# A three-layer edge-convolution kernel: two of the lone group's products between its first nodes, PSUM pools laid in another order, two of the last pairs in plain float32, and a second queue for the last stores

## The chip, the cores and the metric

The kernel runs on one core of one Trainium2 chip. The metric is the device time of one execution in microseconds (us); lower is better. A core has five engines with their own instruction queues: PE (TensorE, matrix products), DVE (VectorE), ACT (ScalarE), POOL (GpSimd) and SP (SyncE, which issues transfers here). They run side by side and wait for each other by semaphores. "PEld" in a profile is PE's load of the stationary operand.

## The reference, cut to what matters

There are 2500 nodes with 256 features and 80000 edges, sorted by their target. A layer is an edge convolution with a mean over a node's incoming edges:

```python
h = jnp.maximum(_layernorm(x), 0.0)
xs = [h]
for W, b in ((W0, b0), (W1, b1), (W2, b2)):
    xi, xj = h[dst], h[src]
    m = jnp.concatenate([xi, xj - xi], axis=-1) @ W + b          # 80000 x 256
    s = segment_sum(m, dst, 2500); cnt = segment_sum(1, dst, 2500)
    h = relu(s / maximum(cnt, 1)[:, None])
    xs.append(h)
return x + jnp.concatenate(xs, axis=-1) @ Wf + bf
```

With A[source, target] the number of edges between two nodes, and W split into an upper half Wa and a lower half Wb, a node's sum is its column of A times (h Wb + b), plus cnt times its own h (Wa - Wb). So nothing has to be done per edge once A is there.

## The kernel before

All of it is in `by_windows` (a general routine, `general`, stands behind a flag that is read at the very end and isn't entered for these inputs). Nodes lie in 20 tiles of 128, taken as Q = 10 pairs. Instructions on the engines stand in the order in which the code issues them (the wrappers `PEo`, `DVEo`, `ACTo`, `SPo` of class `InOrder`, line 282, which is why nearly every line of the profile is L282; the tile names tell the groups apart).

**Start and layer 0 (0 to 206 us).** A list of two-letter acts, `order` (line 893), is run by `perform`: loads, layer norm of node pairs (`st`, `rs`, `sq`, `sc`, `N`: statistics, variance, root, scales, normalization), transposition to feature-major `hT` (`T`, `R`), the search for the edges' blocks (`first`, `next`, `pick`, `pk`, `sg`, `se`, `ge`) and the first products. In `order`, `sc0` is `scales(0)` on DVE and `pick` is `find_rows`, three DVE instructions whose result PE multiplies in `pk`; `warm12` puts twelve idle products on PE ahead of the first `pk`. Then A is built from one-hot products, in five groups of target columns, four of 504 and one of 486 (group 4, the "lone" group), and stored to DRAM as bf16 (`a_dram`), while PE multiplies the previous group.

**Layers 1 and 2.** `hT` holds features times the node's edge count, and `share` is one over the count. Each layer has two stages.

The *node stage* is a loop over i in 0..Q+1 (line 1298). For pair i, `Nodes.multiply` makes 12 products of 128x512 in float32r: per tile, h times [Wb | the layer's part of Wf], where each operand is split in three float32r parts by `Split` (ACT makes the high part, DVE the low one and then the third, "across") and by `Forms` for the weights, and a product is high x high + low x ... + across x ... (`times`). `Nodes.parts` scales the Wb half into `zh` and `zl` (high and low part of z), and `add_to_acc` adds the Wf half to the output sum `acc`. `combine` and `sums` make four combinations of a pair's z. `split(order[i + 2])` makes the split of the next pair but one. Between the pairs, two pairs behind (LAG = 2), `lone.multiply` adds eight products of 128x486 of z with the lone group's counts to two PSUM banks from the pool `ps_two`. `lone.end` closes them with the group's own term: four plain float32 products of `wt` (Wa - Wb) with `hT`, and a ReLU each. The nodes' banks come from the pool `ps_six` (six banks).

The *stream* (70 steps) multiplies z with the four other groups, as two pairs of groups by seven products in place of eight, with banks from both pools in turn. In its last steps (`tick`) the next stage's `Forms` and its first splits are made: for layer 2 those of the first three pairs in the order, for the final stage those of the first four.

**The final stage (457 to 476 us)** is a loop over the pairs in the order 8, 9, 0, 1, 2, 3, 7, 6, 5, 4: 12 products of 128x256 by `times` into the two halves of one bank, two `add_to_acc` on DVE, two stores of 128 rows from SP, and the `split` of a pair some places on. After it, each engine loads the flag `missing` (L1372), branches (L1373) past `general`, and meets the others at closing barriers (L1397).

```python
for i, q in enumerate(order):
    po, sp = bank(), splits.pop(q)
    for k in range(2):
        times(po[:, k * D:(k + 1) * D], sp, k, coming[0])
    for k in range(2):
        t = 2 * q + k
        add_to_acc(t, po[:, k * D:(k + 1) * D])
        n = P if t < NT - 1 else LAST
        SPo.dma_start(out[t * P:t * P + n, :], acc[:n, t, :])
    for k in order[i + 1:i + 4]:
        if k not in splits:
            split(k)
```

Of the kernel before, what the change touches and what calls it, by code (L numbers as in the profile page):

```python
# [12 lines left out]
PSUM = bass.MemoryType.PSUM  # L13
# [300 lines left out]
def by_windows(ctx: ExitStack, tc: tile.TileContext, x, src, dst, Ws, bs, Wf, bf, out, missing):  # L314
    nc = tc.nc
    PE, DVE, ACT, POOL, SP = nc.tensor, nc.vector, nc.scalar, nc.gpsimd, nc.sync
    PEo, DVEo, POOLo, ACTo, SPo = (InOrder(tc, e) for e in (PE, DVE, POOL, ACT, SP))
    P = 128
    N, D = x.shape
# [4 lines left out]
    L = len(Ws)  # L324
    DC = D // P
# [22 lines left out]
    Q = NT // 2  # L348
# [23 lines left out]
    def bank():  # L372
        return ps[-1].tile([P, 512], F32, name="bank")


    acc = const.tile([P, NT, D], F32, name="acc")
    hT = const.tile([P, DC, NP], F32, name="hT")

    zh = const.tile([P, 2, Q * D + 32], F32R, name="zh")
# [17 lines left out]
    lim = const.tile([P, WG], F32, name="lim")  # L397
# [16 lines left out]
    def tile_of(z, t):  # L414
        return z[:, t % 2, t // 2 * D:(t // 2 + 1) * D]
# [20 lines left out]
    ws = [None] * L  # L436
    wfs = [None] * (L + 1)
    raws = [None] * (L + 1)

    def load_wb(l, queue=SP):  # L440
        raws[l] = wpool.tile([P, DC, 2, D], F32, name="wbf", bufs=1)
        ws[l] = wpool.tile([P, DC, D], F32, name="wt"), raws[l][:, :, 0, :]
        queue.dma_start(ws[l][1], Ws[l][D:2 * D, :].rearrange("(c p) d -> p c d", p=P))

    def load_wt(l, queue=SP):
        queue.dma_start(ws[l][0], Ws[l][0:D, :].rearrange("(c p) d -> p c d", p=P))

    def load_wf(l, queue=SP):
        if l == L:
            raws[l] = wpool.tile([P, DC, 2, D], F32, name="wbf", bufs=1)  # L450
        wfs[l] = raws[l][:, :, 1, :]
        queue.dma_start(wfs[l], Wf[l * D:(l + 1) * D, :].rearrange("(c p) d -> p c d", p=P))
# [22 lines left out]
    def load_b(l, queue=SP):  # L475
        queue.dma_start(brow[PAD:PAD + 1, l % 2, :], bs[l].rearrange("(o d) -> o d", o=1))
# [28 lines left out]
    first = pp.tile([P, 1], F32, name="first")  # L505
    after = pp.tile([P, 1], F32, name="after")
    behind = pp.tile([P, WG * P], F32, name="behind")
    pick = pp.tile([P, WG * P], F32R, name="pick")
# [334 lines left out]
    def layer(l, g, a, own, PE=PE, ACT=ACT):  # L843
# [47 lines left out]
        "warm": keep_warm,  # L891
    }
    order = """
        long warm8 lim io first next dstr st0 rs0 sq0 sc0 warm12 N0 pick pk00 sg00 pk01 sg01 st1 T0 pk11 R0 st4 rs1 sq1 pk30 se0
        sg11 sc1 Z0 pk20 N1 st5 sg30 ge0 T1 st6 R1 rs3 F0 sg20 pk21 sq3 st7 pk10 H0 F1 rs4 st3 sq4 sc4 G0 st9
        sc3 L0 sg21 N6 pk31 ka0 kb0 Z1 N5 st8 N7 G1 T6 rs5 sg10 sg31 km0 T5 se1 kt0 R6 H1 st2 F6 sq5 sc5 k10 k20
        rs2 Z6 ge1 L1 T7 B0 R5 R7 Z5 B1 C0 B2 ka1 G6 H6 N9 H5 C1 T9 F7 E0 ge2 kb1 R9 sq2 km1 E1 kt1 C2 B3 k21 Z9
# [39 lines left out]
    splits, coming = {}, []  # L937
# [4 lines left out]
    def flat(l):  # L942
        return raws[l].rearrange("p c t d -> p c (t d)") if l < L else wfs[l]
# [57 lines left out]
    for g in range(NG):  # L1001
        at = {}
        own = LATE
        if g + 1 < NG:
# [5 lines left out]
            if g:  # L1010
                own = [u + 1 - i for i, u in enumerate(sorted(at)[1:5])]
# [20 lines left out]
    first_layer.close()  # L1032

    banks_of.close()
    ps_two = ctx.enter_context(tc.tile_pool(name="ps_two", bufs=2, space=PSUM))
    ps_six = ctx.enter_context(tc.tile_pool(name="ps_six", bufs=6, space=PSUM))
    turn_of = [0]

    def bank():
# [22 lines left out]
    def combine(to, x):  # L1062
        DVEo.tensor_sub(to[:, M3:S5 + 1, :], x[:, 1::2, :], x[:, 0:2, :])
        DVEo.tensor_sub(to[:, S2, :], to[:, M3, :], x[:, 3, :])
        DVEo.tensor_add(to[:, M4, :], to[:, S2, :], x[:, 2, :])
# [4 lines left out]
    def times(to, split, i, forms):  # L1070
        for c in range(DC):
            for k in range(3):
                PEo.matmul(to, split.parts[k][:, c, i * P:(i + 1) * P], forms.parts[k][:, c, :],
                           start=(c == 0 and k == 0), stop=(c == DC - 1 and k == 2))

    def add_to_acc(t, po):
        DVEo.scalar_tensor_tensor(acc[:, t, :], po, share[:, t:t + 1], acc[:, t, :], op0=OP.mult, op1=OP.add)

    class Nodes:
# [4 lines left out]
        def multiply(self, split, forms):  # L1084
            self.banks = [bank(), bank()]
            for i in range(2):
                times(self.banks[i], split, i, forms)
# [117 lines left out]
    class Alone:  # L1205
# [12 lines left out]
        def multiply(self, p):  # L1218
            block = self.blocks.pop(p)
            for i in range(2):  # L1220
                t = 2 * self.order[p] + i
                for o in range(DC):
                    for z in (zh, zl):
                        unit[0] = PEo.matmul(self.to[o], tile_of(z, t)[:, o * P:(o + 1) * P], block[:, i, :self.n],
                                             start=(p == 0 and i == 0 and z is zh), stop=False)

        def end(self):
            for o in range(DC):
                for c in range(DC):
                    PEo.matmul(self.to[o], ws[self.l][0][:, c, o * P:(o + 1) * P],  # L1230
                               hT[:, c, self.c0:self.c0 + self.n], start=False, stop=(c == DC - 1))
            for o in range(DC):
                ACTo.activation(hT[:, o, self.c0:self.c0 + self.n], self.to[o], AF.Relu)

# [2 lines left out]
    def load_alone(k, order):  # L1237
        c = order[2 * k] // 2
        st = stage.tile([P, 8 * GS], BF16, name="staged").rearrange("p (t n) -> p t n", n=GS)[:, :4, :]
        SPo.dma_start(st, a_dram[alone][:, 4 * c:4 * c + 4, :])  # L1240
        loaded[k] = st
# [39 lines left out]
                tick(n)  # L1281

    AHEAD_H = 2
    LAG = 2
    orders = [None, list(range(Q)), [8, 9, 0, 1, 2, 3, 7, 6, 5, 4], [8, 9, 0, 1, 2, 3, 7, 6, 5, 4]]
    def split(q):
        tile_ = stage.tile([P, 4 * GS], F32R, name="staged")
        Split(q, [tile_[:, k * 2 * D:(k + 1) * 2 * D] for k in range(3)])

    for l in range(1, L):  # L1290
        order = orders[l]
        lone = Alone(l, order)
        if l == 1:
            load_alone(0, order)
            split(order[2])
        pending = []
        stream = Stream(l)
        for i in range(Q + LAG):
            if 0 < i <= Q:
                lone.make(i - 1)  # L1300
            if i < Q:
                q = order[i]
                n = Nodes(l, q)
                n.multiply(splits.pop(q), coming[0])
                if i + AHEAD_H < Q and i % 2 == 1:
                    load_alone((i + 1) // 2, order)
                n.parts()
                n.combine()
                if i + AHEAD_H < Q and order[i + AHEAD_H] not in splits:
                    split(order[i + AHEAD_H])  # L1310
                pending.append(n)
            if i and pending:
                pending.pop(0).sums()
            if i >= LAG:
                lone.multiply(i - LAG)
            if i == Q - 1:
                load_alone(Q // 2 - 1, order)
                stream.load(3)
        stream.make(2)
        lone.end()  # L1320
        turn_of[0] = 0
        if l + 1 < L:
            load_b(l + 1, SPo)
            load_wb(l + 1, SPo)
            load_wt(l + 1, SPo)
        load_wf(l + 1, SPo)
        after = orders[l + 1]

        def tick(n):
            if n == 3:  # L1330
                combine(wsum, ws[l][0].rearrange("p c (o n) -> p (c o) n", o=2))
            if n == 40 and l + 1 < L:
                DVEo.tensor_sub(ws[l + 1][0], ws[l + 1][0], ws[l + 1][1])
            if n in (49, 56):
                split(after[(n - 49) // 7])
            if n == 63 and l + 1 < L:
                load_alone(0, after)
            if n in ((65,) if l + 1 < L else (63, 65)):
                split(after[2 + (65 - n) // 2])
            if n == 64:  # L1340
                raw = flat(l + 1)
                coming[:] = [Forms(raw, [raw[:, c, :] for c in range(DC)])]
                coming[0].high()
                coming[0].low()
            if n == 66:
                coming[0].across()
            if n == 67:
                coming[0].last()

        stream.run(tick)  # L1350

    order = orders[L]
    for i, q in enumerate(order):
        po, sp = bank(), splits.pop(q)
        for k in range(2):
            times(po[:, k * D:(k + 1) * D], sp, k, coming[0])
        for k in range(2):
            t = 2 * q + k
            add_to_acc(t, po[:, k * D:(k + 1) * D])
            n = P if t < NT - 1 else LAST  # L1360
            SPo.dma_start(out[t * P:t * P + n, :], acc[:n, t, :])
        for k in order[i + 1:i + 4]:
            if k not in splits:
                split(k)


# [36 lines left out]
```

## Time and profile before

| | |
|---|---|
| Median of 3 runs (lowest, highest) | 483.75 us (483.29, 484.77) |
| Profiled execution: its own time | 483.3 us |
| Its span | 481.5 us |
| Around the span | 1.8 us |
| PE, DVE, ACT, POOL busy | 469.0, 387.5, 303.5, 43.2 us |
| Start and layer 0 | 0 to 206 us |
| Layer 1: node stage, stream | 206 to 249, 249 to 332 us |
| Layer 2: node stage, stream | 332 to 376, 376 to 457 us |
| Final stage, and end of the program | 457 to 476, 476 to 481.5 us |

How to read it: a busy time is the part of the span in which an engine had an instruction under way; matrix products are pipelined, so a row of products that start every 0.23 us may each be shown as 0.39 us long. In lists in order of time, a row has its start, its length, engine, line, operation, the tiles written and read, their shapes and a count; "[0.33 <-DVE staged]" says that the engine was idle for 0.33 us before it and that a DVE instruction on the tile `staged` ended the wait. A "q" behind an engine is its instruction queue: issues of transfers, branches and semaphore waits. The tile `staged` is also what the splits of the later pairs are written to, `block` holds the `Forms` and the counts as float32r, `wbf` the weights Wb and the part of Wf, `pz` the first layer's plain products.

### The profile page before, as it was taken

Reading aid. Unit: us, or ns where it says so; the run is one execution under the profiler, and the core shown is the slowest. Engines: PE = TensorE matmul, PEld = TensorE weight load, DVE = VectorE, ACT = ScalarE, POOL = GpSimd, SP = SyncE. Lnnn points to the kernel's source line nnn. Section 1 sums busy time; section 2 is a strip of 40 time slices with the busy share of each in tenths; the row PEclk is TensorE's granted clock in tenths of the full one; section 3 lists DMA queues with packets and bytes.
Section 4 is the critical chain, followed back from the end, with each engine's and each line's share of the span. In section 5 each row is a group of like instructions: output and inputs, shape, how many; then the busy total and the mean of one; then the engine's idle time right before and its main releaser. Section 6 shows DMA issues by size and latency. Waiting matters only on the chain.

```text
span 481.5 us, 7530 instructions
## 1 busy us (share of the span) xinstructions
PE 469.0 (97%) x2736; PEld 367.8 (76%) x2736; DVE 387.5 (80%) x840; ACT 303.5 (63%) x530; POOL 43.2 (9%) x66
## 2 busy tenths in 40 slices
PE   8999999999999999999999999999999999999993
PEld 4888888677777778777887867877788787688693
DVE  8999988998889884559986838876999586669885
ACT  5676677564644336077868857766877796588340
POOL 3683016100101001000000000000000000000000
PEclk9999999999999999999999999999999999999998
DMA  9310088990641906522186552011124754220033
GB/s 285 111 52 1 2 166 164 197 197 2 128 89 26 189 3 136 100 76 80 43 292 246 174 172 85 3 43 38 49 52 160 283 179 166 86 87 0 2 105 115
DMA packets 21848, 52.76 MB, mean 110 GB/s; under 512 B 1977, under 2 KB 12170, under 8 KB 21770
## 3 DMA queue, kind: packets, MB, share of 16 engines
q1 hardware_dynamic: 15018, 34.57, 21.6%
q0 software_dynamic: 5856, 16.51, 18.0%
q10 hardware_dynamic: 928, 1.11, 0.8%
q8 instruction: 23, 0.38, 0.3%
q14 instruction: 23, 0.19, 0.1%
HBM read 36.72 MB, written 16.10 MB: 110 GB/s over the span
## 4 chain that ended last, share of the span: by engine, by line
PE 88%; DVE 6%; POOL 3%; ACT 1%; issue 1%; DVEq 0%; ACTq 0%; POOLq 0%
PE bank L282 84%; PE pz L282 4%; DVE staged L282 2%; DVE acc L282 2%; POOL acc L282 2%; POOL ed L282 1%; DVE zl L282 1%; POOL es L282 1%; DVE tmp L282 0%; DVE st L282 0%; PE turned L282 0%; ACT zh L282 0%; ACT hT L282 0%; ACT junk L282 0%; DVE mv L282 0%
## 5 line engine op out<-in xcount | busy, mean ns | idle before, releaser
L282 ACT CAST block<-staged 128x1008 fp32r<-128x1008 bf16 x120 | 117.9, 1031 | 16.7 <-DVE staged L282 6.3
L282 ACT CAST a<-bank 128x480 fp32r<-128x480 f32 (+1 forms) x105 | 52.9, 565 | 59.6 <-PE bank L282 59.6
L282 PE MATMUL bank<-a,zh 128*128 128x504 f32 (+1 forms) x200 | 84.3, 421 | 0.0
L282 DVE TENSOR_TENSOR one_m<-iota_m,key_m 128x1024 bf16<-128x1024 bf16 (+1 forms) x105 | 71.8, 684 | 14.2 <-PE bank L282 14.1
L282 PE MATMUL bank<-block,zh 128*128 128x504 f32 (+1 forms) x200 | 82.9, 415 | 0.0
L282 PE MATMUL bank<-a,zl 128*128 128x504 f32 (+1 forms) x200 | 77.8, 389 | 0.0
L282 PE MATMUL bank<-block,zl 128*128 128x504 f32 (+1 forms) x200 | 77.3, 386 | 0.0
L282 PE MATMUL bank<-block,staged 128*128 128x512 f32 (+1 forms) x336 | 69.8, 358 | 1.9 <-DVE staged L282 1.9
L282 PE MATMUL bank<-block,sh 128*128 128x504 f32 x160 | 69.0, 431 | 0.0
L282 DVE TENSOR_TENSOR one_n<-iota_n,key_n 128x480 bf16<-128x480 bf16 (+1 forms) x210 | 66.7, 357 | 0.0
L282 PEld LDWEIGHTS bank<-block,staged 128*128 128x128 f32 x336 | 55.4, 188 | 13.4 <-DVE staged L282 3.9
L282 PE MATMUL bank<-block,sl 128*128 128x504 f32 x160 | 62.6, 391 | 0.0
L282 DVE TENSOR_TENSOR block<-staged 128x1008 fp32r<-128x1008 bf16 x40 | 46.9, 1204 | 5.3 <-PE bank L282 3.9
L282 PEld LDWEIGHTS <-one_m 128*128 128x128 bf16 x834 | 39.1, 98 | 10.0 <-issue 3.2
L282 PEld LDWEIGHTS bank<-a,zh 128*128 128x128 f32 x200 | 37.8, 189 | 10.7 <-issue 2.6
L282 PEld LDWEIGHTS bank<-block,zh 128*128 128x128 f32 x200 | 37.6, 188 | 10.4 <-issue 2.5
L282 PEld LDWEIGHTS bank<-block,zl 128*128 128x128 f32 x200 | 37.6, 188 | 10.3 <-issue 3.2
L282 PE MATMUL bank<-one_n,one_m 128*128 128x120 bf16 x834 | 44.2, 208 | 0.4 <-DVE one_n L282 0.4
L282 PEld LDWEIGHTS bank<-a,zl 128*128 128x128 f32 x200 | 37.7, 189 | 9.0 <-issue 2.6
L282 DVE TENSOR_TENSOR staged<-staged 128x1008 bf16<-128x1008 bf16 x40 | 27.1, 678 | 20.8 <-ACT block L282 20.4
L282 PE MATMUL pz<-wbf,hT 128*128 128x256 f32 x160 | 38.4, 385 | 0.1
L282 PEld LDWEIGHTS bank<-block,sh 128*128 128x128 f32 x160 | 30.1, 188 | 10.4 <-issue 3.5
(152 smaller groups left out, 593.2 us busy)
## 6 DMA issues: line engine op xcount, KB each, us to landing
staged<-a_dram SPq DMA_DIRECT2D x52, 504.0 KB, 4.1
a_dram<-a POOLq DMA_DIRECT2D x20, 630.0 KB, 9.3
out_dram<-acc SPq DMA_DIRECT2D x19, 128.0 KB, 2.0
acc<-in_x_dram POOLq DMA_DIRECT2D x3, 640.0 KB, 11.8
wbf<-in_L_gnn_Wf_dram SPq DMA_DIRECT2D x4, 256.0 KB, 7.3
acc<-in_x_dram SPq DMA_DIRECT2D x1, 896.0 KB, 9.5
acc<-in_x_dram ACTq DMA_DIRECT2D x1, 768.0 KB, 7.1
wbf<-in_L_gnn_W_dram SPq DMA_DIRECT2D x3, 256.0 KB
```

Of the source, the lines that this page charges most:

```text
L282: return self.tc.keep_in_program_order(call(*args, **kwargs))
```

## The change

- In `order`, `pick` moves from behind `sc0` to ahead of it.
- `ps_six` is opened before `ps_two`, so the nodes' banks are the first six and the lone group's the last two.
- Of the lone group's four own products, the two with the first half of the features move from `lone.end` into the node stage: `lone.own(0, 0)` behind the products of the second pair, `lone.own(1, 0)` behind those of the third. They now open the accumulation.
- In the final stage, pairs 2 and 7 (`PLAIN`) are multiplied in plain float32: four products per pair of `hT` with the unsplit `wfs[L]`, and no split is made for them. Because `wfs[L]` has to stay whole, the last `Forms` keeps its rest in the unused half of the weight tile.
- The last pair's two halves get a bank each.
- The second store of each of the last two pairs is issued by ACT, not SP.

```diff
--- before.py
+++ after.py
@@ -891,7 +891,7 @@
         "warm": keep_warm,
     }
     order = """
-        long warm8 lim io first next dstr st0 rs0 sq0 sc0 warm12 N0 pick pk00 sg00 pk01 sg01 st1 T0 pk11 R0 st4 rs1 sq1 pk30 se0
+        long warm8 lim io first next dstr st0 rs0 sq0 pick sc0 warm12 N0 pk00 sg00 pk01 sg01 st1 T0 pk11 R0 st4 rs1 sq1 pk30 se0
         sg11 sc1 Z0 pk20 N1 st5 sg30 ge0 T1 st6 R1 rs3 F0 sg20 pk21 sq3 st7 pk10 H0 F1 rs4 st3 sq4 sc4 G0 st9
         sc3 L0 sg21 N6 pk31 ka0 kb0 Z1 N5 st8 N7 G1 T6 rs5 sg10 sg31 km0 T5 se1 kt0 R6 H1 st2 F6 sq5 sc5 k10 k20
         rs2 Z6 ge1 L1 T7 B0 R5 R7 Z5 B1 C0 B2 ka1 G6 H6 N9 H5 C1 T9 F7 E0 ge2 kb1 R9 sq2 km1 E1 kt1 C2 B3 k21 Z9
@@ -1032,8 +1032,8 @@
     first_layer.close()
 
     banks_of.close()
+    ps_six = ctx.enter_context(tc.tile_pool(name="ps_six", bufs=6, space=PSUM))
     ps_two = ctx.enter_context(tc.tile_pool(name="ps_two", bufs=2, space=PSUM))
-    ps_six = ctx.enter_context(tc.tile_pool(name="ps_six", bufs=6, space=PSUM))
     turn_of = [0]
 
     def bank():
@@ -1222,13 +1222,15 @@
                 for o in range(DC):
                     for z in (zh, zl):
                         unit[0] = PEo.matmul(self.to[o], tile_of(z, t)[:, o * P:(o + 1) * P], block[:, i, :self.n],
-                                             start=(p == 0 and i == 0 and z is zh), stop=False)
+                                             start=False, stop=False)
+
+        def own(self, o, c):
+            PEo.matmul(self.to[o], ws[self.l][0][:, c, o * P:(o + 1) * P],
+                       hT[:, c, self.c0:self.c0 + self.n], start=(c == 0), stop=(c == DC - 1))
 
         def end(self):
             for o in range(DC):
-                for c in range(DC):
-                    PEo.matmul(self.to[o], ws[self.l][0][:, c, o * P:(o + 1) * P],
-                               hT[:, c, self.c0:self.c0 + self.n], start=False, stop=(c == DC - 1))
+                self.own(o, 1)
             for o in range(DC):
                 ACTo.activation(hT[:, o, self.c0:self.c0 + self.n], self.to[o], AF.Relu)
 
@@ -1281,6 +1283,7 @@
                 tick(n)
 
     AHEAD_H = 2
+    PLAIN = (2, 7)
     LAG = 2
     orders = [None, list(range(Q)), [8, 9, 0, 1, 2, 3, 7, 6, 5, 4], [8, 9, 0, 1, 2, 3, 7, 6, 5, 4]]
     def split(q):
@@ -1311,6 +1314,8 @@
                 pending.append(n)
             if i and pending:
                 pending.pop(0).sums()
+            if 0 < i <= DC:
+                lone.own(i - 1, 0)
             if i >= LAG:
                 lone.multiply(i - LAG)
             if i == Q - 1:
@@ -1339,7 +1344,7 @@
                 split(after[2 + (65 - n) // 2])
             if n == 64:
                 raw = flat(l + 1)
-                coming[:] = [Forms(raw, [raw[:, c, :] for c in range(DC)])]
+                coming[:] = [Forms(raw, [raw[:, c, :] if l + 1 < L else raws[L][:, c, 0, :] for c in range(DC)])]
                 coming[0].high()
                 coming[0].low()
             if n == 66:
@@ -1351,16 +1356,22 @@
 
     order = orders[L]
     for i, q in enumerate(order):
-        po, sp = bank(), splits.pop(q)
+        po = bank()
+        po = [po[:, :D], bank()[:, :D] if i == Q - 1 else po[:, D:]]
         for k in range(2):
-            times(po[:, k * D:(k + 1) * D], sp, k, coming[0])
+            if q in PLAIN:
+                for c in range(DC):
+                    PEo.matmul(po[k], hT[:, c, (2 * q + k) * P:(2 * q + k + 1) * P], wfs[L][:, c, :],
+                               start=(c == 0), stop=(c == DC - 1))
+            else:
+                times(po[k], splits[q], k, coming[0])
         for k in range(2):
             t = 2 * q + k
-            add_to_acc(t, po[:, k * D:(k + 1) * D])
+            add_to_acc(t, po[k])
             n = P if t < NT - 1 else LAST
-            SPo.dma_start(out[t * P:t * P + n, :], acc[:n, t, :])
+            (ACTo if i >= Q - 2 and k else SPo).dma_start(out[t * P:t * P + n, :], acc[:n, t, :])
         for k in order[i + 1:i + 4]:
-            if k not in splits:
+            if k not in splits and k not in PLAIN:
                 split(k)
```

## The prediction

> **What bounds the kernel now.** I read the page's busy rows and chain first, then busy time by stage, then the instructions in order of time in the stages that the change touches.
>
> ```profile
> PE 469.0 (97%) x2736; PEld 367.8 (76%) x2736; DVE 387.5 (80%) x840; ACT 303.5 (63%) x530; POOL 43.2 (9%) x66
> PE 88%; DVE 6%; POOL 3%; ACT 1%; issue 1%; DVEq 0%; ACTq 0%; POOLq 0%
> ```
>
> PE is busy 97% and makes 88% of the chain that ended last. A gain must take work from PE, fill one of its holes, or shorten a stretch that PE doesn't own. Busy time by stage (length; then PE, PEld, DVE, ACT, POOL) finds the holes:
>
> ```profile
> 332.00:376.00 44.00, 43.44 (x189) 35.21 (x189) 37.42 (x83) 33.72 (x57) 0.00 (x0) 1.00 0.34 105
> 376.00:457.00 81.00, 81.00 (x326) 60.67 (x325) 59.14 (x82) 58.11 (x68) 0.00 (x0) 1.00 0.31 107
> 457.00:476.00 19.00, 16.27 (x123) 15.03 (x121) 17.04 (x34) 5.66 (x8) 0.00 (x0) 1.00 0.35 115
> 476.00:482.00 6.00, 0.00 (x0) 0.00 (x0) 0.00 (x0) 0.00 (x0) 0.00 (x0) 0.66 0.23 76
> ```
>
> The streams are solid. Layer 2's node stage lacks 0.6, the final stage 2.7, and the last 6 us hold no computing. The node stage's hole, in order of time:
>
> ```profile
> 341.51 0.69 DVE L282 TENSOR_TENSOR staged<-hT,staged 128x512 fp32r<-128x512 f32 x1
> 341.54 0.39 PE L282 MATMUL bank<-block,staged 128*128 128x512 f32 x1
> ...
> 342.23 0.69 DVE L282 SCALAR_TENSOR_TENSOR staged<-staged 128x512 fp32r<-128x512 f32 x1
> ...
> 342.25 0.49 PE L282 MATMUL bank<-block,staged 128*128 128x512 f32 x1 [0.33 <-DVE staged L282]
> ...
> 342.98 0.73 PE L282 MATMUL bank<-block,staged 128*128 128x512 f32 x2 [0.23 <-DVE staged L282]
> ```
>
> The fourth pair's `Split` is late: DVE makes its second and third part as PE asks for them. Starts lie 0.71 and 0.73 apart where 0.23 is the pace: 0.97 lost. The final stage on DVE:
>
> ```profile
> 466.11 0.69 DVE L282 SCALAR_TENSOR_TENSOR staged<-staged 128x512 fp32r<-128x512 f32 x1
> 466.72 0.87 DVE L282 SCALAR_TENSOR_TENSOR acc<-bank,share,acc 128x256 f32<-128x256 f32 x2
> 467.51 0.68 DVE L282 TENSOR_TENSOR staged<-hT,staged 128x512 fp32r<-128x512 f32 x1
> 468.22 0.69 DVE L282 SCALAR_TENSOR_TENSOR staged<-staged 128x512 fp32r<-128x512 f32 x1
> 468.83 0.87 DVE L282 SCALAR_TENSOR_TENSOR acc<-bank,share,acc 128x256 f32<-128x256 f32 x2
> ```
>
> DVE never idles here: a pair costs 2.11 (466.72 to 468.83), 0.78 for two adds and 1.33 for one split, while PE's 12 products take 1.42 (pairs' adds began at 458.96 and 460.38). PE's weight loads wait 0.54 a pair. DVE bounds this stage. Then the end:
>
> ```profile
> L282 SPq DMA_DIRECT2D out_dram<-acc x6: 332/392/1697, 473.6 to 477.3; - x6
> L1373 SPq EVENT_SEMAPHORE  x8: 17/17/17, 478.3 to 479.2; - x8
> L1373 ACTq COMPARE_BRANCH  x1: 50/50/50, 466.9 to 466.9; - x1
> L1373 ACTq EVENT_SEMAPHORE  x1: 17/17/17, 469.6 to 469.6; - x1
> L1397 SPq DRAIN  x3: 7/7/131, 480.4 to 480.9; - x3
> ```
>
> The six last stores queue on SP; one issue took 1.70, so the last went out at 477.3, though DVE's last add began at 475.1 (call it R). SP's wait for landings ends at 479.2, it reaches the closing barrier at 480.4 to 480.6, and the span ends at 481.5, R+6.4. ACT had left long before.
>
> **What the Trainium skill says.** "FP8 and Floating Point Precision", TensorE Precision Notes: true float32 takes four passes. The trace agrees: the chain has the eight 128x256 records of a float32 `product` in 1.73, 0.43 per product, against 0.117 for a float32r one, 3.7 times. "DMA: Bandwidth & Descriptors", Issuing engines are not separate DMA queues: a second issuing engine only saves the sequencer's time to initiate, usually small. Here that time is 0.3 to 0.4, once 1.70. "Runtime: NRT & Kernel Launch", Instruction fetch mechanics: a taken branch out of the loaded window waits for a DMA fetch. The trace agrees: ACT's branch takes 0.05 but its next instruction comes 2.7 later; DVE's comes 3.1 later, and PE's branch alone takes 4.0. "PSUM — Partial Sum Buffer", PSUM bank collisions: two engines must not touch one bank at once; accordingly a pair's two adds follow all twelve products here.
>
> **The change, part by part.**
>
> *Lone group's own products.* In each of two layers, two of four float32 products move from `end` to behind the second and third pair of nodes. Each is two records 0.41 apart, 0.81 (eight in 202.11 to 205.5). PE's total stays. In layer 2 they put 1.63 ahead of the fourth pair, which then starts at 341.54+1.63 = 343.17; its parts are ready at 342.25 and 342.98. The split's inputs come from pair 1, whose products precede the moved ones, so DVE isn't later. The hole closes: **-1.0**. Behind the products on PE stand pair 3 and the lone group's products; their readers on DVE and ACT are 0.8 to 1.6 later once, and catch up because a node costs PE 12x0.234+8x0.22 = 4.57 and DVE some 4.4. What the products read (`wt`, lone columns of `hT`) was finished before the stage. In layer 1 no such hole shows: 0, since the two nodes given before are taken from `end`. Range -1.1 to -0.7 if a later split is late instead.
>
> *PSUM banks.* The first pair now lands in a bank that layer 0's last group held. PE waits for that group's last ReLU at 206.20 already (0.67), and the built program's semaphore wait is the same; the other banks were emptied before. 0, from -0.1 to +0.2.
>
> *Start.* `find_rows` (0.15+0.49+0.75, some 1.2 in all) goes ahead of `scales` on DVE. `pick` is ready at 7.4 instead of 7.9, but PE's warm-up products hold it to 8.4: nothing gained. `normalize` of pair 0 on ACT moves from 6.60 to about 7.8 and ends at 8.9, just when PE wants it (8.90) and ACT wants `count_half` (8.95). 0, from -0.1 to +0.2.
>
> *Two plain pairs.* Pairs 2 and 7, fifth and seventh in the order, lose their splits (2x1.33 on DVE, 2x0.63 on ACT) and cost PE 1.73 instead of 1.42. Follow it in the old clock: the fourth pair ends on PE at 460.34+2x1.42 = 463.18, the fifth (plain) at 464.91. DVE, done before that with the split of pair 3, runs from 464.95 without a hole: three times (two adds 0.78, one split 1.33) is 6.33, then six adds 0.39 apart; the last starts at 464.95+6.33+1.95 = 473.23 against 475.08. PE finishes pairs at 466.3, 468.1, 469.5 and 470.9, each before DVE wants it; the last waits about 0.3 for its split. **-1.8.** At a plain pair of 1.9 it is -1.6; at worst I allow -1.2. The rest of the last `Forms` now lies in an unused half of the weight tile: same instructions, 0. The last pair's second bank lets its first add start early, but DVE is behind there: 0 to -0.1.
>
> *Two queues.* Of six last stores ACT issues two. The last goes out at R+0.5 on ACT instead of R+2.3 on SP. With a landing of 2.0 to 3.4 (medians of all stores, and of the last six) it lands at R+2.5 to 3.9, against R+4.1: 0.2 to 1.6 earlier. But ACT can only leave after its own last issue: 0.5+0.4 issue+0.5 load of the flag+2.7 to 4.0 fetch puts it at the barrier at R+4.2 to 5.5, where SP stood at R+5.4. So at most -1.2, at least +0.1; I take **-0.9**. ACT has nothing else queued behind these stores.
>
> Sum: -1.0-1.8-0.9 = -3.7. The profiled execution took 483.3, so 479.6; it lies 0.45 under the median of 483.75, so the median is about **480.0**. All unknowns at their good end give 479.3, at their bad end about 482.1.
>
> **Rivals.** *ACT leaves last*: its fetch competes with the stores and eats the two queues' gain: -2.8, **480.9**. PE's 4.0 speaks for it, ACT's own 2.7 against. *The hole only moves*: DVE is 37.4 of 44 busy in that stage, so a later split could be late in place of the fourth; then 0 for the first part, **481.0**. Against it: from there on PE is the slower of the two per node. *The exit turns slower*: the same fetch, behind six stores, takes so long that everything waits for ACT. ACT stands at the barrier at R+1.5 plus that fetch: past 3.9 the queues' gain is gone, at 6.7 the whole gain, and at 8.5 everything waits for ACT until R+10.0, 4.6 later than SP's old 5.4, less the 2.8 won before: **485.5**, slower. Nothing in the trace is over 4.0. That the float32 pairs don't run at the price of the row is unlikely: the shape, types and operands are those of `product`.
>
> **How the numbers follow.** The likeliest case 0.75 (480.0), ACT last 0.14, the hole moved 0.08, exit slower 0.03. About 0.3%, 1.45 us, is what a measurement tells from no change, so faster means under 482.3: all of the first three but their worst corners, 0.91; same 0.06; slower 0.03. The range 479.0 to 482.0 takes in both bounds and the first two rivals.
>
> **What would show it.** Right: no PE wait on `staged` near 342; the float32 records of a plain pair 1.7 to 1.9 long; DVE solid from the fifth pair on with four splits; last add about 2.8 earlier (472.3); span end 5.3 to 5.6 after it. Wrong: waits on `staged` later in the node stage, PE idle before the sixth or eighth pair, an ACT branch whose next instruction comes over 4 after it, or PE later than 8.5 at the first `pick` product.

## The result, and the profile after

| | before | after |
|---|---|---|
| Median of 6 runs (lowest, highest) | 483.18 us (482.29, 484.77) | 479.73 us (479.23, 480.56) |
| Ratio of after to before, 95% interval | | 0.9926 [0.9908, 0.9945] |
| Profiled execution: its own time, span | 483.3, 481.5 us | 480.26, 478.5 us |

The median falls by 3.45 us. The forecast was a gain of 3.7 and a time of 480.0, counted from the 483.75 of the first three runs; errors of opposite sign in it partly cancel. The page of the changed kernel, busy rows and chain:

```profile
PE 468.4 (98%) x2728; PEld 367.8 (77%) x2728; DVE 386.2 (81%) x836; ACT 302.5 (63%) x528; POOL 43.1 (9%) x66
PE 90%; DVE 4%; POOL 3%; ACT 1%; issue 1%; DVEq 0%; POOLq 0%; ACTq 0%
```

PE's share of the chain is up from 88 to 90%, DVE's down from 6 to 4. Busy time by stage (length; then PE, PEld, DVE, ACT, POOL), the stages moved by the 1 us that they now start earlier:

```profile
331.00:375.00 44.00, 44.00 (x191) 35.58 (x190) 36.82 (x80) 33.39 (x56) 0.00 (x0) 1.00 0.30 93
456.00:473.00 17.00, 15.61 (x115) 14.70 (x113) 14.59 (x30) 4.51 (x6) 0.00 (x0) 1.00 0.39 127
473.00:479.00 6.00, 0.00 (x0) 0.00 (x0) 0.00 (x0) 0.00 (x0) 0.00 (x0) 0.62 0.25 80
```

Layer 2's node stage has no hole left (43.44 before), and PE stands idle for 1.4 in the final stage's stretch instead of 2.7. The last 6 us are as empty as they were. The place of the old hole, in order of time:

```profile
340.67 0.98 PE L282 MATMUL bank<-hT,wt 128*128 128x486 f32 x2
...
341.60 0.68 DVE L282 TENSOR_TENSOR staged<-hT,staged 128x512 fp32r<-128x512 f32 x1
...
342.32 0.69 DVE L282 SCALAR_TENSOR_TENSOR staged<-staged 128x512 fp32r<-128x512 f32 x1
...
343.25 2.02 PE L282 MATMUL bank<-block,staged 128*128 128x512 f32 x8
```

DVE writes the fourth pair's second and third part when it did before, but PE is held by an own product at 340.67 and the lone group's eight, and starts the pair at 343.25. Nothing waits. DVE in the final stage:

```profile
463.96 0.88 DVE L282 SCALAR_TENSOR_TENSOR acc<-bank,share,acc 128x256 f32<-128x256 f32 x2 [0.17 <-PE bank L282]
464.75 0.68 DVE L282 TENSOR_TENSOR staged<-hT,staged 128x512 fp32r<-128x512 f32 x1
...
469.69 0.69 DVE L282 SCALAR_TENSOR_TENSOR staged<-staged 128x512 fp32r<-128x512 f32 x1
470.30 2.44 DVE L282 SCALAR_TENSOR_TENSOR acc<-bank,share,acc 128x256 f32<-128x256 f32 x6
```

The fifth pair's adds wait 0.17 for PE; from there DVE runs without a break to six adds in a row, the last at R = 472.26. Then the end: the last stores, and the branches past `general` (line 1384 now):

```profile
L282 SPq DMA_DIRECT2D out_dram<-acc x4: 333/392/1552, 470.8 to 472.4; - x4
L282 ACTq DMA_DIRECT2D out_dram<-acc x2: 372/762/1151, 472.0 to 472.8; - x2
...
DMA to landing us min/median/max: 3.4/3.5/3.6
L1384 SPq EVENT_SEMAPHORE  x8: 17/17/17, 474.5 to 476.3; - x8
L1384 PEldq COMPARE_BRANCH  x1: 4002/4002/4002, 471.1 to 471.1; - x1
L1384 ACTq COMPARE_BRANCH  x1: 54/54/54, 474.5 to 474.5; - x1
...
L1384 ACTq EVENT_SEMAPHORE  x1: 17/17/17, 477.4 to 477.4; - x1
```

The last stores go out at R+0.1 on SP and R+0.5 on ACT, as forecast, but both issues are long (1.55 and 1.15) and end together at R+1.66. The two stores whose landing the trace shows (two of those before the last two) land 3.4 and 3.6 us after their issue, and SP's wait for landings ends at 476.3, R+4.0, where it ended at R+4.1 before. ACT branches at 474.5 and its next instruction comes at 477.4: it is last at the barrier, and the span ends at R+6.2, against R+6.4.

### The profile page after: what moved, and what is told of

It reads as the page before. It is cut to its first block, busy times and chain, and to the rows that moved or that the text cites. A ratio compares the mean times of both kernels' runs of the same rounds, so it can differ in the third digit from the quotient of the medians.

```text
span 478.5 us, 7510 instructions
## 1 busy us (share of the span) xinstructions
PE 468.4 (98%) x2728; PEld 367.8 (77%) x2728; DVE 386.2 (81%) x836; ACT 302.5 (63%) x528; POOL 43.1 (9%) x66
## 4 chain that ended last, share of the span: by engine, by line
PE 90%; DVE 4%; POOL 3%; ACT 1%; issue 1%; DVEq 0%; POOLq 0%; ACTq 0%
PE bank L282 87%; PE pz L282 3%; POOL acc L282 2%; DVE acc L282 1%; DVE staged L282 1%; POOL ed L282 1%; ACT junk L282 1%; POOL es L282 1%; DVE st L282 0%; DVE one_m L282 0%; ACT hT L282 0%; PE turned L282 0%; DVE zl L282 0%; DVE one_n L282 0%; DVE mv L282 0%
## 5 line engine op out<-in xcount | busy, mean ns | idle before, releaser
L282 PE MATMUL bank<-block,staged 128*128 128x512 f32 (+1 forms) x312 | 66.5, 364 | 0.3 <-DVE staged L282 0.3
L282 PEld LDWEIGHTS bank<-block,staged 128*128 128x128 f32 x312 | 52.5, 188 | 10.8 <-DVE staged L282 0.5
```

The lines of the kernel that those rows point to most:

```text
L282: return self.tc.keep_in_program_order(call(*args, **kwargs))
```

## The experiments

All are edits of the changed kernel. Their times carry intervals of 1 us and more, so the stages of their profiles tell more. The table follows one DVE instruction each through the profiles, as shifts against the profile of before: one at the end of layer 0 (206.70 there), then what layer 1's node stage (to one at 257.06) and layer 2's (to 386.06) add. "Adds" is from the first to the last add of the final stage, "end" from the last add R to the end of the span.

| kernel | layer 0 | layer 1 | layer 2 | adds | end | median | ratio to before, 95% |
|---|---|---|---|---|---|---|---|
| before | 0 | 0 | 0 | 16.11 | 6.39 | 483.18 | |
| changed | +0.38 | -0.30 | -1.08 | 14.32 | 6.19 | 479.73 | 0.9926 [0.9908, 0.9945] |
| u_queue | -0.06 | -0.29 | -1.09 | 14.32 | 6.28 | 480.45 | 0.9919 [0.9896, 0.9942] |
| u_plain | -0.41 | -0.29 | -1.09 | 16.04 | 7.07 | 482.22 | 0.9948 [0.9927, 0.9968] |
| u_own | +0.18 | 0.00 | 0.00 | 14.30 | 6.03 | 481.36 | 0.9931 [0.9908, 0.9953] |
| u_start | +0.05 | -0.29 | -1.08 | 14.32 | 5.90 | 480.35 | 0.9908 [0.9885, 0.9931] |
| stay3 | +0.39 | -0.29 | -1.08 | 14.33 | 5.59 | 479.79 | 0.9899 [0.9875, 0.9924] |
| stay3_swap | +0.15 | -0.29 | -1.08 | 14.32 | 6.55 | 479.62 | 0.9895 [0.9870, 0.9921] |
| stay3_one | -0.36 | -0.29 | -1.09 | 14.32 | 6.84 | 480.08 | 0.9904 [0.9878, 0.9929] |
| plain3 | +0.10 | -0.29 | -1.09 | 13.74 | 6.30 | 480.16 | 0.9905 [0.9879, 0.9931] |
| again | +0.31 | -0.29 | -1.08 | 14.32 | 5.75 | 479.39 | 0.9885 [0.9854, 0.9916] |
| plain3_one | -0.14 | -0.29 | -1.09 | 13.74 | 7.50 | 480.69 | 0.9916 [0.9883, 0.9948] |
| plain3_swap | -0.25 | -0.29 | -1.08 | 13.74 | 5.41 | 479.33 | 0.9886 [0.9855, 0.9917] |
| stay8 | +0.51 | -0.29 | -1.08 | 14.32 | 6.94 | | |

The u rows, the stay3 and plain3 rows, and the last four were each measured as one set (plain3 with the stay3 rows). Among kernels with the same code in a stage, the columns layer 1, layer 2 and adds repeat to 0.02 or so (adds without plain pairs to 0.07); layer 0 and the end wander. Both have to be known before a term of a few tenths is read off one execution.

**u_own: the own products back in `end`.**

```diff
-            if 0 < i <= DC:
-                lone.own(i - 1, 0)
...
-                self.own(o, 1)
+                for c in range(DC):
+                    self.own(o, c)
```

> The changed kernel with all four own products back in end and the start flag back on the lone group's first product. Theory A: two holes come back, 1.09 in layer 2's node stage near 342 and 0.29 in layer 1's near 217, where the trace of before has two starts of PE's second pair 0.42 and 0.34 apart against a pace of 0.23, inside a merged row; R is 1.4 later, time 481.1. Rival B, the term on record: layer 2's 1.0 alone, 480.7. Rival C: the 0.29 of layer 1 belongs to the new order of the PSUM banks and not to the products; then layer 1's stage stays as short as it is and only layer 2's changes.

Both holes come back, and nothing else: 0.00 in each layer where the change has -0.29 and -1.08. Layer 2's, in order of time:

```profile
341.72 0.39 PE L282 MATMUL bank<-block,staged 128*128 128x512 f32 x1
...
342.43 0.50 PE L282 MATMUL bank<-block,staged 128*128 128x512 f32 x1 [0.32 <-DVE staged L282]
...
343.16 1.20 PE L282 MATMUL bank<-block,staged 128*128 128x512 f32 x4 [0.22 <-DVE staged L282]
```

So theory A holds, and the banks' order (new here) has no part in layer 1's gain. That gain could have been read from the profile of before, whose row in order of time for layer 1's fourth pair is this (three pairs of 12 products and eight of the lone group's stand before it, from 206.20 on):

```profile
216.36 2.32 PE L282 MATMUL bank<-block,staged 128*128 128x512 f32 x8
```

The same pair in the changed kernel:

```profile
218.36 2.50 PE L282 MATMUL bank<-block,staged 128*128 128x512 f32 x10
```

Neither shows a wait. But 8 products in 2.32, the last 0.40 long, start (2.32-0.40)/7 = 0.274 apart, and 10 in 2.50 start 0.233 apart: seven intervals 0.041 too long on the mean, 0.29 in all. In the records two of them are long, 0.42 and 0.34. Pipelined products overlap, so the row closes over a start that is late by less than a product's length.

**u_plain: no plain pairs.**

```diff
-    PLAIN = (2, 7)
+    PLAIN = ()
```

> The changed kernel with no plain pairs (PLAIN empty: all ten pairs of the final stage by splits). Theory A: DVE bounds the final stage at 2.11 a pair; first add to last add goes from 14.32 back to 16.12, R comes 1.8 later, PE waits for staged in each of the last six pairs, and the time is 479.7+1.8 = 481.5. Rival B: part of the 1.8 comes from the own products having cleared DVE's way; then the stage gets longer by only 1.0 to 1.4: 480.9. Nothing moves before 457 us.

The adds take 16.04, 1.72 more, which is A and not B. PE waits for `staged` again, in four waits rather than the six expected:

```profile
PE bank L282 <- DVE staged L282: 1.4, 4, 0.3
```

In the changed kernel that row of the waits has 0.3 in one. The span end at R+7.1 is another matter: ACT's next instruction came 3.7 after its branch here.

**u_queue: all stores on SP.**

```diff
-            (ACTo if i >= Q - 2 and k else SPo).dma_start(out[t * P:t * P + n, :], acc[:n, t, :])
+            SPo.dma_start(out[t * P:t * P + n, :], acc[:n, t, :])
```

> The changed kernel (479.73 us, last add R, span end R+6.2) with all stores on SP again. Theory A, from the two traces: ACT's exit eats the second queue's gain, and PE's instruction fetch of 16 KB (1.48 us at 472.1) holds one of the 16 DMA engines while the last stores are issued, whichever queue issues them; then one SP issue takes about 1.7, the last store goes out near R+2.3 and the span ends at R+6.4 as before the change: +0.2 us, 479.9, with ACT gone long before. Rival B, the term on record: the second queue is worth 0.9, so span end at R+7.1 and 480.6. Rival C: with ACT gone early and its fetch out of the way the end comes no later than with two queues: 479.5.

The stores in the last stretch, and the branches:

```profile
L282 SPq DMA_DIRECT2D out_dram<-acc x6: 333/390/1444, 470.4 to 473.9; - x6
L1384 SPq EVENT_SEMAPHORE  x8: 17/17/17, 474.9 to 475.7; - x8
...
L1384 ACTq COMPARE_BRANCH  x1: 50/50/50, 462.4 to 462.4; - x1
```

With R = 471.84 the last store goes out at R+2.1, ACT has left nine microseconds earlier, one issue takes 1.44, SP's wait for landings ends at R+3.9 and the span at R+6.28. That is theory A. Its median, 480.45, lies nearer rival B's 480.6 than A's 479.9; but u_start, measured in the same set with both queues, took 480.35, so the times don't speak for B. The four kernels with the changed kernel's two queues and no extra work on PE (u_plain, u_own, u_start, again) end at R+5.75 to R+7.07. By these executions the second queue is worth 0.1 or 0.2 to this kernel, below what this end does by itself.

**u_start: the old start order.**

```diff
-        ... rs0 sq0 pick sc0 warm12 N0 pk00 ...
+        ... rs0 sq0 sc0 warm12 N0 pick pk00 ...
```

> The changed kernel with find_rows behind scales again (order of before). In the profiled execution of the changed kernel layer 0 is 0.38 us longer than before; the 0.43 arise between 36 and 38 us, where two DVE instructions of away take 0.57 and 0.52 instead of 0.35 and 0.36 beside a POOL that runs acc meanwhile faster. Theory A: that comes of the new start order, so it goes when the order is undone: layer 0 ends 0.4 earlier (last ReLU of hT near 206.2), time 479.3. Rival B: it is chance from one execution to the next, found with either order: time 479.7, and layer 0 in the other kernels that keep the new order ends sometimes at 206.2 and sometimes at 206.6.

Layer 0 ends at +0.05, which alone would speak for A. But the twelve profiles with the new order end it anywhere from -0.41 to +0.51, 0.07 later than before on their mean; rival B. What differs at 36 us, DVE before:

```profile
36.24 0.35 DVE L282 TENSOR_SCALAR away<-ed,below 128x256 bf16<-128x256 int32 x1
36.63 0.36 DVE L282 SCALAR_TENSOR_TENSOR away<-away 128x128 bf16<-128x128 bf16 x1
```

and after:

```profile
36.30 0.57 DVE L282 TENSOR_SCALAR away<-ed,below 128x256 bf16<-128x256 int32 x1
36.91 0.52 DVE L282 SCALAR_TENSOR_TENSOR away<-away 128x128 bf16<-128x128 bf16 x1
```

The same two instructions take 0.38 longer, while POOL's updates of `acc` beside them take less than before. The new order doesn't bring this with it: in seven of the twelve profiles with that order the two take 0.34 to 0.37, as in both with the old one, and layer 0 ends at -0.41 to +0.15; in the other five they take 0.49 to 0.57, and it ends at +0.18 to +0.51. Whether the order makes the longer form more likely can't be told from so few. That the two engines hinder each other there is a guess; no run took POOL's work away.

**stay3, stay3_swap, stay3_one: PE leaves later.** Why are the last issues long? Three float32 products that nobody reads keep PE 0.84 longer (its branch at R-0.34 in place of R-1.18):

```diff
+    for _ in range(3):
+        PEo.matmul(bank()[:, :D], hT[:, 0, :P], wfs[L][:, 0, :], start=True, stop=True)
```

> The changed kernel with three more float32 128x256 products on PE behind its last pair (they go to a bank that nobody reads), 1.3 us at 0.43 each, so that PE's exit and its 16 KB instruction fetch start at about R+1.1 instead of R-0.2. Theory A: the fetches hold one of the 16 DMA engines, and a store's packets on that engine wait; that gave the long issues (1.55 and 1.15) and kept SP's last landing at R+3.9 to 4.1 with one queue or two. With the fetch later the last issues take 0.33 to 0.40, SP's last landing comes at R+2.4 to 3.2, and the end is set by ACT's or PE's exit at R+4.2 to 4.6: span end R+5.1 to 5.5 instead of R+6.2, time about 0.9 lower than the changed kernel's: 478.8, or a ratio near 0.9907 to the kernel before. Rival B: a later fetch of PE only puts the fetches of DVE, ACT and PE into another order on the same DMA engine, and the end stays at R+5.9 to 6.3: 479.7. Rival C: PE itself leaves last, at R+2.8+1.3 plus more wait: R+5 or later, end R+6 to 6.5, 479.9.

The 16 KB fetch moved to R+0.8, the last issues took 0.33 and 0.35, and the span ended at R+5.6, 0.1 above theory A's range. But the last landing, at R+3.8, hardly moved: the fetch no longer held up the issues, it held up the stores' packets instead. u_start shows the same without any change to PE's work: there the fetch began only at R+0.6, the last issues took 0.33 and 0.35, SP's wait for landings still ended at R+4.1, and the span at R+5.9. Why the fetch came later there isn't known. The second kernel also gives ACT the earlier store of each pair:

```diff
-            (ACTo if i >= Q - 2 and k else SPo).dma_start(...)
+            (ACTo if i >= Q - 2 and not k else SPo).dma_start(...)
```

> As the kernel with PE's three more products, and ACT issues the first store of each of the last two pairs in place of the second, so ACT's last issue is 0.39 earlier and SP has the last one. Theory A: where ACT's exit set the end, the end comes up to 0.39 earlier than in that kernel, until PE's exit near R+4.2 sets it: span end R+5.0 to 5.2, 478.5. Rival B: SP, with the last store, is last by its landing (issue at R+0.1, landing 2.3 to 3.9 later): end R+5.5 or later, no gain over the other. Rival C: the fetches set the end and nothing changes: R+5.9 to 6.3.

ACT is at the barrier at R+4.3 as before, but SP's last landing comes at R+4.8 behind a fetch of 1.77, and the span ends at R+6.55: rival B. In the third, all stores are on SP:

> As the kernel with PE's three more products, and all stores on SP, ACT gone long before. Theory A: the six stores go out 0.475 apart, the last at R+0.95, and land at R+3.3; SP's closing waits take 0.85 more, R+4.2, about when PE's exit ends: span end R+5.1 to 5.3. So one queue is as good as two once PE's fetch is out of the way, 478.6. Rival B: the second queue matters then: 0.4 to 0.9 later than with it.

The last of six went out at R+0.9, as expected, but that issue itself took 1.85, behind the fetch that began at R+0.9: R+6.84. That is 1.25 later than with two queues, past rival B's 0.4 to 0.9 (the medians differ by 0.29), and the fetch made it, not the number of stores on the queue. All three missed theory A's time. Moving the fetch changes which store it hits.

**stay8: the fetch behind all stores.** The same edit with `range(8)`.

> The changed kernel with eight more float32 products on PE behind its last pair, so that PE's branch and its 16 KB fetch come after all stores have been moved (fetch at R+2 or later). One look, for the landing alone. Theory A: the landing at R+3.8 to 4.1 is made by PE's fetch on a DMA engine that carries a share of every store; without it the last issues take 0.33 to 0.40 and SP's last landing comes at R+2.3 to 2.9. Rival B: a store's landing takes 3.5 us and more here by itself or by the other engines' fetches: last landing still at R+3.5 or later. The end is PE's own exit by either, at R+5.5 to 6.5, span end R+6.4 to 7.4.

The last stores:

```profile
L282 SPq DMA_DIRECT2D out_dram<-acc x4: 332/358/394, 470.9 to 472.5; - x4
L282 ACTq DMA_DIRECT2D out_dram<-acc x2: 350/356/363, 472.1 to 472.9; - x2
...
DMA to landing us min/median/max: 1.8/1.9/1.9
```

There is one execution of it, so its time isn't compared. No issue is long, and the stores whose landing the trace shows land in 1.8 to 1.9 instead of 3.4 to 3.6. The transfers of 2.4 us from R-0.3, in 40 slices of 60 ns (GB/s, then the packets of PE's fetch, q8, and the others'), in the changed kernel:

```profile
GB/s 478 86 154 290 324 358 324 273 205 103 120 222 341 324 375 358 291 291 376 290 307 307 290 171 52 17 0 17 0 17 154 0 17 0 17 0 34 17 17 34
...
q8 instruction: 1, 0.02, 3.9%
q14 instruction: 1, 0.01, 0.8%
```

and in stay8:

```profile
GB/s 256 154 120 222 324 341 358 324 324 171 69 205 290 358 393 341 342 376 308 342 358 358 324 325 290 342 358 341 375 308 307 308 495 307 461 256 188 69 0 34
...
q14 instruction: 2, 0.02, 2.6%
```

That q8 is PE's fetch is read from its start, which follows PE's branch by 0.9 to 1.3 in every profile but u_start's (1.8), wherever that branch is moved. The single packet of q8 takes 3.9% of 16 engines' 2.4 us, 1.5 us of one engine. From 1.4 us into the stretch on, the changed kernel moves almost nothing: what is left of the earlier stores trickles out packet by packet, as from a single engine. (The packets don't name their engine; that it is one is read from the rate.) The last two stores, whose issues end at R+1.66, aren't in this stretch at all: they move from R+2.2 to R+3.1. Without the fetch they move within it, and nearly all is done by R+1.9. That is theory A's mechanism, though SP's wait for the landings ended only at R+3.4, between A's 2.9 and B's 3.5: three 8 KB fetches by the other engines fell in R+1.6 to R+3.0, and the last packets of ACT's store trickle beside them.

**plain3, plain3_swap, plain3_one: a third plain pair, the last.**

```diff
-    PLAIN = (2, 7)
+    PLAIN = (2, 7, 4)
```

> The changed kernel with the last pair (4) plain too: PLAIN = (2, 7, 4). It takes one split of 1.33 us from DVE (and 0.63 from ACT) and adds 0.31 to PE. Theory A: with two plain pairs the stage is about balanced: PE's 10 pairs are 8x1.42+2x1.73 = 14.8, DVE's first to last add 14.3; with a third PE's time is 15.1 and it finishes its last product about 0.0 to 0.1 later than now (0.31 more, 0.28 less of waiting for the last split), DVE has no backlog, and R moves from 472.26 to about 472.0 on the same start: gain 0.1 to 0.3, time 479.5. Rival B: DVE still bounds the stage: 1.33 less, 478.4. Rival C: PE bounds it already: 0.3 later, 480.0.

The stage is 0.58 shorter, twice what theory A gave and less than half of B's. DVE's last rows:

```profile
467.93 3.11 DVE L282 SCALAR_TENSOR_TENSOR acc<-bank,share,acc 128x256 f32<-128x256 f32 x7
471.41 0.48 DVE L282 SCALAR_TENSOR_TENSOR acc<-bank,share,acc 128x256 f32<-128x256 f32 x1 [0.38 <-PE bank L282]
```

DVE has caught up before the end and waits 0.38 for PE's very last product: PE bounds the stage now, and with DVE's queue gone only one add is left behind PE. Theory A had overlooked that two adds stood there, 0.33 of the 0.58. The rest is PE's: its last product ends 0.25 sooner after the stage's first add. A charged PE 0.31 for the third plain pair and took off a wait of 0.28, but in the changed kernel two of the last pair's starts lie 0.56 and 0.22 apart where 0.12 is the pace, so the wait that went was 0.54. The span still ended only at R+6.3. The two other divisions of the stores, first the swap as above:

> Pairs 2, 7 and 4 plain, and ACT issues the first store of each of the last two pairs in place of the second; so ACT's last issue comes about 0.86 earlier against R (the last two adds were 0.86 apart). Theory A: ACT's exit, last before at R+5.3, comes at R+3.6 to 4.5, SP has the last store and lands at R+2.5 to 3.5, DVE leaves at R+3.8 to 5.1: span end R+4.8 to 6.0, time 0.6 to 1.4 under the changed kernel's. Rival B: the fetches set the end: R+6.2, 0.6 under it.

The end, R+5.41, fits theory A. But the median is 479.33, against 479.39 of the unaltered kernel in the same set: neither theory's gain of 0.6 shows in it. And one queue:

> Pairs 2, 7 and 4 plain, and all stores on SP. With three plain pairs the stage was 13.74 from first to last add (0.58 shorter), since the last pair's first add no longer stands behind DVE's last split, and PE's exit was over by R+1.4; what stayed last was ACT's and DVE's exit (R+5.1 to 5.3). Theory A: with one queue ACT is gone at R-7, SP's last issue goes out at about R+0.5 to 1.4 and lands at R+3 to 3.9, DVE leaves at R+3.8 to 5.1: span end R+5.2 to 6.0, R 0.58 earlier; time 0.6 to 1.2 under the changed kernel's on this chip. Rival B: the fetches take their time in any order and the end stays at R+6.2: 0.6 under it. Rival C: one queue of six stores makes SP last at R+6.3 or later: 0.4 under it.

R+7.5 and 480.69, later than even rival C had it. The fetch came at R-1.6 and held up one of the last stores for 1.8, and four more then queued behind it on SP. Here the second queue matters: plain3_swap, of the same set, takes 479.33, and the times of the two don't overlap (plain3, in another set, took 480.16).

**again: the changed kernel once more.** No edit.

> The changed kernel itself, unaltered, beside the others of this set, so that they can be compared on one chip. If layer 0's length and the exit vary by chance, this execution's shifts against the kernel before differ from the first profile of it: at the end of layer 0 anything from -0.4 to +0.4 instead of +0.38, and the span end anywhere from R+5.9 to R+7.1. What must stay the same: layer 1's node stage 0.29 shorter, layer 2's 1.09 shorter, 14.32 from the first to the last add of the final stage. Ratio near 0.9926.

The middle columns repeat to 0.01 and the end moves by 0.44. Its time, 479.39, agrees with the first 479.73, yet the ratio is 0.9885 against 0.9926, because the kernel before took 485.15 in this set (482.96 to 486.21) where it took 483.18 in the first: a gain of 5.8 here and 3.45 there. In all three later sets its runs lie either at 483.0 to 483.9 or at 484.7 to 486.2. What makes it slower there isn't settled; it wasn't profiled again. No version tried beats the changed kernel by more than the runs' own spread.

## Why the prediction was right, point by point

| Term | Forecast | Measured |
|---|---|---|
| Own products, layer 2 | -1.0 | -1.08 |
| Own products, layer 1 | 0 | -0.29 |
| Banks and start (layer 0) | 0 | +0.38 in the profiled execution, +0.07 on the mean of twelve |
| Two plain pairs | -1.8 | -1.80; -1.72 by u_plain |
| Two queues | -0.9 | -0.20; -0.1 by u_queue |
| Sum | -3.7 | -3.0 in the profiled execution; -3.3 with the mean for layer 0 |

*Lone group's own products.* Right in layer 2: the pair starts at 343.25 (343.17 forecast), and no later split is late. The 0.08 more is a third late start, 0.34 after the second, which the prediction's 0.97 left out. Wrong in layer 1: "in layer 1 no such hole shows: 0" was read from merged rows. u_own settles it.

*Banks and start.* 0 stands for the start, whose order can't be told from chance: PE's first `pick` product begins at 8.39, where 8.42 was before, though `normalize` moves from 6.60 to 7.46. PE's wait for layer 0's last ReLU, at the start of layer 1, is 0.67 in both profiles, so the banks cost nothing there; their order was not run alone.

*Two plain pairs.* Right in each step. A plain pair and the next split pair together take 3.14 on PE (1.73+1.42 forecast); the fifth pair's adds start at 463.96, which is the 464.95 of the old clock less 1.0; the last add is at 472.26, forecast 472.3 (here layer 0's +0.38 and layer 1's -0.30, neither of them forecast, happen to cancel). "FP8 and Floating Point Precision" of the Trainium skill (TensorE Precision Notes) put the price at four passes, the record that the prediction used measured it at 3.7, and 3.7 held.

*Two queues.* This term is mis-sized. The failing step is "it lands at R+2.5 to 3.9, against R+4.1": it landed at R+4.0. The prediction took the long issue of 1.70 for a property of SP's queue, which a second queue would get round. It was PE's exit: PE's instruction fetch starts about R-0.2 in both profiles, since PE's last product keeps its distance from the last add, and the stores issued then wait for it on either queue. ACT's last issue, counted as 0.4, took 1.15 for the same reason. The bound from ACT's exit (R+4.2 to 5.5; its terms as written sum to 4.1 to 5.4) held, R+5.2, and ACT does leave last, the rival given 0.14. But taking ACT off the path (u_queue) gains nothing, so that rival has the order of events right and not the cause. "DMA: Bandwidth & Descriptors" (Issuing engines are not separate DMA queues) says that transfers from all issuing engines run on the same 16 DMA engines and that a second issuer saves only the time to initiate, usually small; the prediction quoted it and then priced more. For this change the runs agree with the page: 0.1 to 0.2. With a third plain pair that time isn't small: one queue took 1.36 more than plain3_swap by the medians, and in its trace one issue of 1.80, during PE's fetch, kept four others waiting.

*Fetches.* "Runtime: NRT & Kernel Launch" (Instruction fetch mechanics) says that a fetch goes through DMA in blocks of 16 KiB; the records show 16 KB and 8 KB packets. From branch to next instruction it took 2.5 to 3.7 on ACT, 2.9 to 4.3 on DVE, and PE's branch took 3.7 to 4.6. The forecast's 2.7 to 4.0 for ACT was a little high at both ends.

Of the forecast gain of 3.7 the medians show 3.45: the queues were put 0.7 too high, and the own products gave 0.4 more than forecast. That these two nearly make up for each other is luck. The prediction's bad ends, summed again, give a gain of 1.4 and 482.35 rather than 482.1; either lies outside the range of 479.0 to 482.0, which was said to take in both bounds.

## What to carry to other kernels

Divide a merged row of pipelined products by its count before calling a stage solid: 0.274 a start where 0.233 is the pace is a hole without a wait. When two engines take turns at bounding a stage, trade work until both end together, and then count what stands behind the last product. Before a store is moved to another queue, ask whether the queue is late or the transfer: the instruction fetches of engines that leave the program run on the same DMA engines as the last stores.

## What the hardware showed that was not expected

- A fetch of 16 KB took 0.9 to 1.8 us as one packet. Stores issued shortly before it or during it landed in 3.0 to 3.6 instead of 1.8 to 1.9 (where the traces show a landing), and an issue held up by it took 0.8 to 1.85 instead of 0.33 to 0.40, on SP and ACT alike. Not every issue that falls into it is held: ACT's first one in plain3 and plain3_swap took 0.37 in the middle of the fetch.
- From the last add to the end of the span, the same program took 5.75 and 6.19 in two executions, and layer 0's length differed by up to 0.9 between kernels whose first 206 us are the same work.
